# A routed-expert kernel whose residual copy of x is made from HBM to HBM, eight batches later, with SyncE's order written out

## The chip, the cores and the metric

The kernel runs on one core of a Trainium2 chip. Its time is the device time of one execution in microseconds (us). All arithmetic is in float32.

## What is computed

The input x has 32 batches of 128 tokens with 1024 channels. Two blocks follow each other, each added to its input. The first mixes the tokens of each batch with a 128x128 matrix that is looked up by the batch's condition, and sends the result through a mixture of 64 experts, 8 for each token. The second is a linear map with a low-rank adapter for each batch, followed by another linear map with a router over 8 low-rank experts.

```python
w = weights[conditions]
h = jnp.einsum('bct,bcd->bdt', x, w)
...
probs = jax.nn.softmax(h @ gate_w.T)
w, sel = jax.lax.top_k(probs, 8)
...
h = silu(einsum('ech,ehi->eci', inp, wg)) * einsum('ech,ehi->eci', inp, wu)
out = jnp.einsum('eci,eih->ech', h, wd)
y = zeros.at[tok].add(g)
...
x = x + moe(h)
x = x + L1_ffn(L1_cond(x))
```

Each expert takes at most 256 tokens. The sum x + moe(h) is what matters here: it is formed in a buffer in HBM.

## The kernel before, in words

There are three stages.

**First stage, 0 to about 283 us.** It works through the 32 batches in 8 groups of 4. For each batch `mixed` multiplies x with the looked-up matrix (two products with 512 columns, called ph), copies them to an SBUF tile h (ACT the left half, VectorE the right half), and ACT issues the write of h to the HBM buffer hbuf. For each group `scored` multiplies the turned x (xTb, loaded from a transposed copy of x) with the gate's weights (64 products, pxg), `logits` and `weights_of` choose 8 experts for each token, and `counted` ranks the tokens of each expert and writes the ranks to HBM. Between groups TensorE also works off the products of two head matrices of the last stage (`combined`, pcw): one in groups 1 to 5, two in groups 6 and 7, then nine more after the groups. During these last nine, `looked_up`, `fetched` and `found` read the ranks back (GpSimd's rkg), find the tokens of the first experts, and TensorE turns the result with a small product (prow).

The buffer ybuf is where the result x + moe(h) grows. It first gets x: `carried(b)` (L373) writes the tile of x of batch b, which is in SBUF for `mixed`, to ybuf. ACT issues this, one batch after the batch's product. Rows past the last token of hbuf, ybuf and ranks get pads: zeros and a constant, written by ACT after group 0.

The tiles: x has 6 buffers, so `loaded_batch(b + 6)` (L330) uses the buffer of batch b. xTb has 4 buffers, one group: `scored(g)` (L342) issues the loads of group g + 1. h has 3.

**Second stage, to about 2146 us.** For each of the 64 experts the kernel loads wg, wu and wd (1.5 MB each), gathers the tokens' rows of hbuf, forms the expert with a scheme of seven products in place of eight (t and s are sums of blocks of weights and tokens), and adds the weighted outputs to the rows of ybuf by an indirect DMA that accumulates.

**Third stage.** The rest of the head products (pcw with WB_b), sums of the combined map BM on VectorE, and then 16 pairs of batches: ybuf is read back (xq), turned (X), multiplied, and the output is written.

**What sets the order.** The program is written with a tile framework. A scheduler orders the instructions of an engine by its own estimate of when they are ready, except those that went through `kept` (L196): these stay in the order of the program. The class `InOrder` (L200) wraps an engine so that all of its instructions are kept. Before, VectorE, TensorE, ACT and GpSimd have such a wrapper (`dve`, `pe`, `act`, `pool`, L208), and SyncE has none: its DMA issues are placed by the scheduler. Instructions that wait hold up everything behind them on their engine. The DMAs that SyncE and ACT issue use eight completion semaphores in turn, so a DMA is issued only when the one that used the semaphore before it has landed.

Of the kernel before, what the change touches and what calls it, by code (L numbers as in the profile page):

```python
# [17 lines left out]
P = 128  # L18
NB = 32
# [32 lines left out]
def kernel(  # L52
# [22 lines left out]
    nc = tc.nc  # L75
# [8 lines left out]
    ybuf = dram.tile([NT + P, H], F32, name="ybuf")  # L84
# [90 lines left out]
    def head_block(n):  # L175
        lo, hi = BLOCKS[n]
        hw = wts.tile([P, HC * BW], F32, name=f"hw_{n}", tag="wg")
        hw = hw[:, 0 : HC * (hi - lo)].rearrange("p (j o) -> p j o", j=HC)
        nc.sync.dma_start(hw, head_w[:, lo:hi].rearrange("(j p) o -> p j o", p=P))
        return hw  # L180

    def left_block(u, k, tag):
        wb = wts.tile([P, 3, HC, P], F32, name=f"WB_{u}_{k}", tag=tag)
        nc.sync.dma_start(wb, WB[:, 3 * k : 3 * k + 3, :, :])
        return [wb[:, d, :, :] for d in range(3)]

    def multiplied(n, d, hw, left, pool, tag, pe):
# [17 lines left out]
            op = getattr(self.engine, name)  # L205
            return lambda *args, **kw: kept(op(*args, **kw))  # L206

    dve, pe, act, pool = (InOrder(e) for e in (nc.vector, nc.tensor, nc.scalar, nc.gpsimd))  # L208

# [21 lines left out]
    def fetched(some, count):  # L233
        if some["rk"] is None:
            some["rk"] = fs.tile(
                [P, some["n"] * NJ, 2, P], F32, name=f"rkg_{some['u']}", tag="rkg", bufs=2
            )
        for s in range(some["got"], some["got"] + count):
            kept(
                nc.gpsimd.indirect_dma_start(  # L240
                    out=some["rk"][:, s, :, :].rearrange("p i t -> p (i t)"),
                    out_offset=None,
                    in_=ranks.rearrange("e b i t -> (e b) (i t)"),
                    in_offset=bass.IndirectOffsetOnAxis(
                        ap=some["row"][:, s // NJ, s % NJ : s % NJ + 1], axis=0
                    ),
                )
            )
        some["got"] += count
# [67 lines left out]
    with (  # L317
# [6 lines left out]
        xs, xTs, ws = {}, {}, {}  # L324

        def loaded_turned(b):
            xTs[b] = a6.tile([P, HC, P], F32, name=f"xTb_{b}", tag="xTb", bufs=4)
            nc.sync.dma_start(xTs[b].rearrange("p j c -> p (j c)"), x_t[b])

        def loaded_batch(b):  # L330
            ws[b] = a6.tile([P, P], F32, name=f"w_{b}", tag="w_b")
            pool.indirect_dma_start(
                out=ws[b],
                out_offset=None,
                in_=cond_w,
                in_offset=bass.IndirectOffsetOnAxis(ap=cond_rows[:, b : b + 1], axis=0),
            )
            xs[b] = a6.tile([P, H], F32, name=f"x_{b}", tag="x_t")
            nc.sync.dma_start(xs[b], x[b])


        def scored(g):  # L342
            pxg = pa_sm.tile([P, GB, E], F32, name=f"pxg_{g}", tag="sm")
            for t in range(GB):
                xT_b = xTs.pop(g * GB + t)
                for j in range(HC):
                    pe.matmul(
                        pxg[:, t, :],
                        xT_b[:, j, :],
                        gw_sb[:, j, :],  # L350
                        start=(j == 0),
                        stop=(j == HC - 1),
                    )
            xg = a2.tile([P, GB, E], F32, name=f"xg_{g}", tag="xg")
            dve.tensor_copy(xg, pxg)
            for b in range((g + 1) * GB, min((g + 2) * GB, NB)):
                loaded_turned(b)
            return xg

        def mixed(b):  # L360
            rows = slice(b * P, (b + 1) * P)
            h_sb = a2.tile([P, H], F32, name=f"h_{b}", tag="h_sb", bufs=3)
            for n in range(2):
                cols = slice(n * 512, (n + 1) * 512)
                ph = pa_big.tile([P, 512], F32, name=f"ph_{b}_{n}", tag="big")
                pe.matmul(ph, ws[b], xs[b][:, cols], start=True, stop=True)
                if n == 0:
                    act.copy(h_sb[:, cols], ph)
                else:
                    dve.tensor_copy(h_sb[:, cols], ph)  # L370
            act.dma_start(hbuf[rows, :], h_sb)

        def carried(b):  # L373
            act.dma_start(ybuf[b * P : (b + 1) * P, :], xs.pop(b))

        def logits(g, xg):
            plog = pa_sm.tile([P, GB, E], F32, name=f"plog_{g}", tag="sm")
            for t in range(GB):  # L380
                pe.matmul(plog[:, t, :], ws[g * GB + t], xg[:, t, :], start=True, stop=True)
            top = a2.tile([P, GB, K], F32, name=f"top_{g}", tag="top")
            left = a2.tile([P, GB, E], F32, name=f"left_{g}", tag="left")
            for t in range(GB):
                dve.max(top[:, t, :], plog[:, t, :])
                dve.match_replace(left[:, t, :], top[:, t, :], plog[:, t, :], LOW)
            nmax = a2.tile([P, GB], F32, name=f"nmax_{g}", tag="nmax")
            dve.tensor_scalar(nmax, top[:, :, 0], -1.0, None, ALU.mult)
            ex = a2.tile([P, GB, E], F32, name=f"ex_{g}", tag="ex")
            for t in range(GB):  # L390
                act.activation(ex[:, t, :], plog[:, t, :], AF.Exp, bias=nmax[:, t : t + 1])
            mask = a2.tile([P, GB, E], F32, name=f"mask_{g}", tag="mask")
            dve.tensor_scalar(mask, left, LOW, None, ALU.is_equal)
            return ex, mask

        def weights_of(g, ex, mask):
            wt = a2.tile([P, GB, E], F32, name=f"wt_{g}", tag="wt")
            dve.tensor_tensor(wt, ex, mask, ALU.mult)
            wsum = a2.tile([P, GB], F32, name=f"wsum_{g}", tag="wsum")
            dve.tensor_reduce(wsum, wt, AX.X, ALU.add)  # L400
            rsum = a2.tile([P, GB], F32, name=f"rsum_{g}", tag="rsum")
            dve.reciprocal(rsum, wsum)
            dve.tensor_tensor(wt, wt, rsum.unsqueeze(2).to_broadcast([P, GB, E]), ALU.mult)
            return wt
# [22 lines left out]
        def combined(n, d):  # L427
            lo, hi = BLOCKS[n]
            halves = multiplied(n, d, hws[n], lefts, pa_big, "big", pe)
            next(halves)  # L430
            yield
            pcw = next(halves)
            if d < HC:
                cw = fs.tile([P, BW], F32, name=f"cw_{n}_{d}", tag="cw", bufs=3)[:, 0 : hi - lo]
                act.copy(cw, pcw)
                act.dma_start(cwbuf[:, d, lo:hi], cw)
            else:
                act.copy(G_sb[:, lo:hi], pcw)
            yield

        gw_sb = a1.tile([P, HC, E], F32, name="gw_sb")
        loaded_turned(0)
        nc.sync.dma_start(gw_sb.rearrange("p j e -> p (j e)"), gate_w)
        for b in range(1, GB):
            loaded_turned(b)
        for b in range(6):
# [8 lines left out]
        NG = NB // GB  # L455
# [4 lines left out]
        for g in range(NG):  # L460
            ex, mask = logits(g, xg)
            for t in range(GB):
                b = g * GB + t
                mixed(b)
                if b:
                    carried(b - 1)
                if t == 1:
                    wt = weights_of(g, ex, mask)
                if b + 6 < NB:
                    loaded_batch(b + 6)  # L470
            if g == 0:
                for buf in (hbuf, ybuf):
                    act.dma_start(
                        buf[NT : NT + P, :].rearrange("p (n c) -> p n c", c=256),
                        zeros.unsqueeze(1).to_broadcast([P, H // 256, 256]),
                    )
                act.dma_start(ranks[:, NB, :, :], pad)
            for _ in range((0, 1, 1, 1, 1, 1, 2, 2)[g]):
                for _ in combined(*rest.pop(0)):
                    pass  # L480
            if g + 1 < NG:
                xg = scored(g + 1)
                if g == 0:
                    lefts += left_block("a", 1, "wd")
                    lefts += left_block("a", 2, "wu")
                if g == 4:
                    hws[1] = head_block(1)
            counted(g, mask, wt)
        part = {0: looked_up([0, 1, 2, 3])}
        fetched(part[0], 4 * NJ)  # L490
        carried(NB - 1)
        gathers = {}
        for d in range(HC + 1):
            step = combined(1, d)
# [419 lines left out]
    hw = head_block(2)  # L914
# [54 lines left out]
    for q in range(NQP):  # L969
# [18 lines left out]
        o = [c3.tile([P, H], F32, name=f"out{t}_{u}", tag=f"out{t}", bufs=2) for t in range(2)]  # L988
# [105 lines left out]
```

## Time and profile before

| what | value |
|---|---|
| median of 3 runs | 2776.29 us (2773.67 to 2780.71) |
| profiled execution: time, span | 2778.05 us, 2776.3 us |
| TensorE busy | 2733.0 us, 98% |
| VectorE, ACT, GpSimd busy | 57%, 15%, 40% |
| bytes moved | 585.10 MB, mean 211 GB/s |
| load of x: issues, size, time to landing | 32, 512 KB, 7.1 us |
| write of x to ybuf | 32, 512 KB, 7.8 us |
| pads of hbuf and ybuf, time to landing | 17.4 and 19.5 us |

A profile shows one execution. The span is the time between its first and last record; the execution's own time is 1.75 us longer. Busy times of an engine are shares of this span, but matmuls are pipelined and the end of one is modelled, so a busy TensorE can be one that runs at a lower clock. "PEclk" is the clock granted to TensorE, in tenths. "DMA" is the mean busy share of the 16 DMA engines. PE is TensorE's matmul, PEld its weight load, DVE VectorE, POOL GpSimd, SP SyncE; SPq and ACTq are issues of DMAs on these engines' queues. A bracket at the end of a line gives the idle time before the instruction and what ended it.

### The profile page before, as it was taken

The numbers are of one execution on the slowest core, as the hardware profiler recorded it, in microseconds if no ns is written. First come the engines' busy times: TensorE is split into PE (matmuls) and PEld (weight loads), VectorE is DVE, ScalarE is ACT, GpSimd is POOL, SyncE is SP. The second block draws the span as 40 slices with busy tenths as digits, with TensorE's granted clock in tenths as the row PEclk, the third lists the DMA queues.
The fourth block names the chain that finished last, engine by engine and source line by source line (L and its number), as shares of the span: only waits on it lengthen the run. The fifth ranks groups of instructions, "written<-read, shape, count | busy, mean of one in ns | idle before, by whom it ended". The sixth has DMA issues, their size and how long they took to land.

```text
span 2776.3 us, 23659 instructions
## 1 busy us (share of the span) xinstructions
PE 2733.0 (98%) x8580; PEld 1515.0 (55%) x8580; DVE 1580.4 (57%) x2521; ACT 408.1 (15%) x792; POOL 1110.6 (40%) x846
## 2 busy tenths in 40 slices
PE   8899999999999999999999999999999899999999
PEld 5666555555555555555555555555555555555554
DVE  2225667666676665766757667576563444444443
ACT  1111111111111111111111111112111000000000
POOL 2114465564655646556465565555451100000000
PEclk9899999999999999999999999999999999999999
DMA  9996687777887778777777787777775522222210
GB/s 348 379 388 231 227 253 253 237 249 229 252 258 229 249 236 249 253 229 247 248 244 248 233 248 254 238 244 238 236 251 154 132 67 62 65 63 60 63 46 38
DMA packets 134724, 585.10 MB, mean 211 GB/s; under 512 B 23312, under 2 KB 50000, under 8 KB 109264
## 3 DMA queue, kind: packets, MB, share of 16 engines
q1 hardware_dynamic: 70112, 388.40, 37.9%
q0 software_dynamic: 51200, 155.24, 24.1%
q10 hardware_dynamic: 13296, 39.95, 3.7%
q8 instruction: 68, 1.11, 0.2%
q14 instruction: 48, 0.39, 0.0%
HBM read 459.68 MB, written 123.83 MB: 210 GB/s over the span
## 4 chain that ended last, share of the span: by engine, by line
PE 94%; DMA 3%; DVE 1%; issue 1%; ACT 0%; ACTq 0%; SPq 0%; POOL 0%; DVEq 0%; POOLq 0%
PE pp L591 41%; PE po L690 23%; PE pr_c L206 17%; PE pcw L206 4%; PE px L206 2%; PE pxg L206 2%; PE pth L641 2%; PE ph L206 1%; DMA xTb<-in_x_t 1%; DMA ybuf<-zeros 1%; PE prk L206 1%; DMA ybuf<-x 1%; DMA wu<-in_wu 0%; PE pg L206 0%; PE pt L206 0%
## 5 line engine op out<-in xcount | busy, mean ns | idle before, releaser
L304 POOL DMA_INDIRECT xin<-hbuf,slot_row x512 | 711.8, 1390 | 156.0 <-issue 152.7
L690 PE MATMUL po<-wd,hTb 128*128 128x512 f32 x1536 | 680.3, 592 | 0.6 <-ACT hTb L643 0.6
L701 POOL DMA_INDIRECT ybuf<-o,slot_tok x128 | 205.2, 1603 | 674.4 <-ACT o L699 472.3
L690 PEld LDWEIGHTS po<-wd,hTb 128*128 128x128 f32 x1536 | 286.8, 190 | 323.6 <-issue 306.1
L591 PE MATMUL pp<-wg,xT 128*128 128x384 f32 x1024 | 351.5, 486 | 0.0
L591 PE MATMUL pp<-t,s 128*128 128x384 f32 x1024 | 342.0, 487 | 0.0
L591 PEld LDWEIGHTS pp<-t,s 128*128 128x128 f32 x1024 | 193.5, 190 | 141.9 <-issue 23.0
L206 DVE TENSOR_TENSOR u<-p,pp 128x384 f32<-128x384 f32 x64 | 35.4, 553 | 392.0 <-PE pp L591 381.8
L591 PEld LDWEIGHTS pp<-wg,xT 128*128 128x128 f32 x1024 | 189.7, 190 | 118.9
L699 ACT ACTIVATE o<-po,slot_w 128x512 f32<-128x512 f32 x256 | 175.9, 687 | 494.2 <-PE po L690 492.1
L206 POOL DMA_INDIRECT ab<-in_AT,adapter_rows x32 | 36.5, 1142 | 447.3 <-ACT pxw L206 441.9
L206 PE MATMUL pr_c<-BM,X 128*128 128x512 f32 x480 | 213.7, 592 | 0.0
L206 DVE STREAM_TRANSPOSE xT<-xin 128x1024 f32<-128x1024 f32 x128 | 155.5, 1232 | 62.1 <-DMA xin<-hbuf,slot_row 53.5
L591 PE MATMUL pp<-wu,xT 128*128 128x384 f32 x512 | 175.6, 486 | 0.0
L591 PE MATMUL pp<-t,xT 128*128 128x384 f32 x512 | 175.6, 486 | 0.0
L591 PE MATMUL pp<-wu,s 128*128 128x384 f32 x512 | 175.6, 486 | 0.0
L608 ACT ACTIVATE h<-gate 128x384 f32<-128x384 f32 x128 | 67.0, 524 | 700.5 <-DVE gate L206 700.4
L240 POOL DMA_INDIRECT rkg<-ranks,row x128 | 123.3, 964 | 88.0 <-DMA ranks<-rk 49.3
L206 PE MATMUL pr_c<-ts,ss 128*128 128x512 f32 x320 | 142.5, 592 | 1.3 <-DVE ss L206 1.3
L206 PEld LDWEIGHTS pr_c<-BM,X 128*128 128x128 f32 x480 | 88.9, 190 | 100.2 <-issue 99.9
L206 DVE TENSOR_TENSOR u<-u,pp 128x384 f32<-128x384 f32 x128 | 70.5, 551 | 125.0 <-PE pp L591 124.9
L591 PEld LDWEIGHTS pp<-wu,xT 128*128 128x128 f32 x512 | 97.3, 190 | 67.8
(158 smaller groups left out, 2924.7 us busy)
## 6 DMA issues: line engine op xcount, KB each, us to landing
wu<-in_wu SPq DMA_DIRECT2D x64, 1536.0 KB, 9.6
wg<-in_wg SPq DMA_DIRECT2D x64, 1536.0 KB, 6.9
wd<-in_wd SPq DMA_DIRECT2D x64, 1536.0 KB, 6.9
xTb<-in_x_t SPq DMA_DIRECT2D x32, 512.0 KB, 7.6
x<-in_x SPq DMA_DIRECT2D x32, 512.0 KB, 7.1
hbuf<-h ACTq DMA_DIRECT2D x32, 512.0 KB, 8.2
ybuf<-x ACTq DMA_DIRECT2D x32, 512.0 KB, 7.8
xq<-ybuf SPq DMA_DIRECT2D x64, 256.0 KB, 5.1
```

Source lines behind the costliest of these rows:

```text
L206: return lambda *args, **kw: kept(op(*args, **kw))
L240: nc.gpsimd.indirect_dma_start(out=some["rk"][:, s, :, :].rearrange("p i t -> p (i t)"), out_offset=None, in_=ranks.rearrange("e b i t -> ...
L304: nc.gpsimd.indirect_dma_start(out=xin[:, q, :], out_offset=None, in_=quarters, in_offset=bass.IndirectOffsetOnAxis(ap=slot_row[:, s : s + ...
L591: nc.tensor.matmul(bank, left[k][:, j, :], right[k][:, j, :], start=(j == 0), stop=(j == HH - 1))
L608: nc.scalar.activation(h, gate, AF.Sigmoid)
L641: nc.tensor.transpose(pt[:, i, :], h[:, i * P : (i + 1) * P], ident)
L690: nc.tensor.matmul(po, hT[j][:, i, :], wd_sb[:, i, cols], start=(i == 0), stop=(i == IC - 1),)
L699: nc.scalar.mul(o_sb[:, cols], po, slot_w[:, s : s + 1])
L701: nc.gpsimd.indirect_dma_start(out=ybuf, out_offset=bass.IndirectOffsetOnAxis(ap=slot_tok[:, s : s + 1], axis=0), in_=o_sb, in_offset=None ...
```

## The change

`carried(b)` no longer writes the SBUF tile: SyncE issues a DMA that copies x[b] in HBM to the rows of ybuf in HBM. The compiled form of one copy is 16 rows of 32 KB each. The tile of x in SBUF then has only the two products as readers. The call moves from one batch after the product to eight batches after, behind the load of batch b + 6; the last eight follow after the groups. The pads are written after group 6 (NG - 2) instead of group 0. SyncE gets an `InOrder` wrapper, and the loads of the turned x, of x, of the gate's weights, of the head blocks and of the WB blocks go through it. The loads of wg, wu and wd, of the small constants, of pxw, BM, xq and the output writes stay outside it.

```diff
-        nc.sync.dma_start(hw, head_w[:, lo:hi].rearrange("(j p) o -> p j o", p=P))
+        sync.dma_start(hw, head_w[:, lo:hi].rearrange("(j p) o -> p j o", p=P))
...
-        nc.sync.dma_start(wb, WB[:, 3 * k : 3 * k + 3, :, :])
+        sync.dma_start(wb, WB[:, 3 * k : 3 * k + 3, :, :])
...
-    dve, pe, act, pool = (InOrder(e) for e in (nc.vector, nc.tensor, nc.scalar, nc.gpsimd))
+    dve, pe, act, pool, sync = (
+        InOrder(e) for e in (nc.vector, nc.tensor, nc.scalar, nc.gpsimd, nc.sync)
+    )
...
-            nc.sync.dma_start(xTs[b].rearrange("p j c -> p (j c)"), x_t[b])
+            sync.dma_start(xTs[b].rearrange("p j c -> p (j c)"), x_t[b])
...
-            nc.sync.dma_start(xs[b], x[b])
+            sync.dma_start(xs[b], x[b])
...
         def carried(b):
-            act.dma_start(ybuf[b * P : (b + 1) * P, :], xs.pop(b))
+            sync.dma_start(ybuf[b * P : (b + 1) * P, :], x[b])
...
-        nc.sync.dma_start(gw_sb.rearrange("p j e -> p (j e)"), gate_w)
+        sync.dma_start(gw_sb.rearrange("p j e -> p (j e)"), gate_w)
...
                 mixed(b)
-                if b:
-                    carried(b - 1)
                 if t == 1:
                     wt = weights_of(g, ex, mask)
                 if b + 6 < NB:
                     loaded_batch(b + 6)
-            if g == 0:
+                if b >= 8:
+                    carried(b - 8)
+            if g == NG - 2:
                 for buf in (hbuf, ybuf):
                     act.dma_start(
                         buf[NT : NT + P, :].rearrange("p (n c) -> p n c", c=256),
...
         fetched(part[0], 4 * NJ)
-        carried(NB - 1)
+        for b in range(NB - 8, NB):
+            carried(b)
         gathers = {}
```

The instruction lists of the two kernels agree on TensorE, VectorE and GpSimd. ACT loses the 32 writes of x, SyncE gains 32 copies. On SyncE's queue four loads of x now stand ahead of four loads of turned x in every group; 15 copies stand one after the other behind the last load of x; the second head block moves behind the turned x of group 6, expert 0's wu behind its wg and the copies; and in the third stage the third WB_b block moves from ahead of the pxw and BM loads to behind them.

## The prediction

> **What bounds the kernel now.** I read the slices of the page first, then busy times cut at the group boundaries of the first stage, then the waits of SyncE's queue, then the order of time at the two places where another engine holds TensorE.
>
> ```profile
> PE   8899999999999999999999999999999899999999
> ...
> PEclk9899999999999999999999999999999999999999
> DMA  9996687777887778777777787777775522222210
> GB/s 348 379 388 231 227 253 253 237 249 229 252 258 229 249 236 249 253 229 247 248 244 248 233 248 254 238 244 238 236 251 154 132 67 62 65 63 60 63 46 38
> ```
>
> One slice is 69.4 us. In the first three the DMA engines are full and TensorE is not; later TensorE is full and the DMAs have room. Only the first 240 us and one dip (slice 32, near 2180 us) can give anything back.
>
> Cut where each group's logits begin (columns: stretch, length, then busy us and instructions of PE, PEld, DVE, ACT, POOL; TensorE's clock, DMA share, GB/s):
>
> ```profile
> 21.00:42.80 21.80, 20.57 (x106) 14.76 (x106) 7.67 (x27) 3.16 (x8) 3.84 (x4) 1.00 0.79 286
> 42.80:78.50 35.70, 30.14 (x124) 20.80 (x125) 6.70 (x23) 5.85 (x13) 3.77 (x4) 0.81 1.03 417
> 78.50:113.30 34.80, 27.84 (x126) 21.06 (x124) 7.50 (x28) 4.80 (x11) 3.89 (x4) 0.80 1.00 392
> 113.30:136.20 22.90, 22.90 (x128) 16.52 (x126) 7.77 (x29) 4.79 (x11) 3.89 (x4) 1.00 0.92 334
> 136.20:163.80 27.60, 26.00 (x122) 18.73 (x121) 7.20 (x26) 4.80 (x11) 3.90 (x4) 0.88 1.00 386
> 163.80:186.30 22.50, 22.50 (x122) 15.81 (x120) 7.50 (x27) 4.27 (x11) 3.89 (x4) 1.00 1.02 390
> 186.30:214.40 28.10, 28.10 (x142) 19.63 (x141) 7.50 (x27) 5.71 (x13) 1.88 (x2) 1.00 0.89 346
> ```
>
> These are groups 0 to 6. Group 5, with one head product and no stall, takes 22.5 us: that is TensorE's own price of a group. Group 1 takes 13.2 us more, group 2 12.3, group 4 5.1: 30.6 us lost, with the DMA share at 1.0. Group 6 has two head products (5.2 us more) and loses nothing.
>
> The waits of SyncE's queue from 20 to 160 us (total, times, longest), and TensorE's place of waiting in group 2:
>
> ```profile
> SPq L339 <- DMA ybuf<-x: 57.2, 10, 10.8
> ...
> 102.08 7.09 PE L206 MATMUL pxg<-gw_sb,xTb 128*128 128x64 f32 x32 [6.96 <-DMA xTb<-in_x_t]
> ```
>
> SyncE stands still for 57 us because the next load of x (L339) may not overwrite a tile of x until that tile has been written to ybuf. Behind it in the same queue stand the turned tiles xTb, which TensorE then lacks.
>
> Two places where order decides, the end of the first stage and the seam before the last:
>
> ```profile
> 235.09 0.46 ACTq L206 DMA_DIRECT2D ranks<-rk  x1
> ...
> 248.60 0.39 PE L206 MATMUL prow<-byq,spread 128*128 128x8 f32 x2 [0.49 <-DVE byq L206]
> ```
> ```profile
> 2146.66 0.33 SPq L184 DMA_DIRECT2D WB_b<-in_WB  x1
> ...
> 2157.84 4.09 SPq L921 DMA_DIRECT2D BM<-cwbuf  x4
> ...
> 2169.55 6.46 DVE L206 SCALAR_TENSOR_TENSOR BM<-chan,own,BM 128x640 f32<-128x640 f32 x8 [6.79 <-DMA BM<-cwbuf]
> ...
> 2184.93 7.38 PE L206 MATMUL px<-pxw,X 128*128 128x152 f32 x32 [12.49 <-issue]
> ```
>
> From the last ranks write to the prow product nothing is spare (0.49 us already lost). At the seam TensorE idles 12.49 us behind VectorE, which waited 6.79 us for BM.
>
> **What the Trainium skill says.** "DMA: Bandwidth & Descriptors", section "Issuing engines are not separate DMA queues": transfers started by SP, ACT and POOL run on the same 16 engines and interleave; the trace agrees (417 GB/s with three queues active, no more). So moving the copy from ACT to SP frees no bandwidth by itself. Same page, "Queues, rings and completion order": an engine alternates between queues packet by packet; no run here shows it. Same page, "Latency and other measured facts", row on HBM row pitch: copies between HBM tensors at full rate are given as 214 GB/s per direction. The trace of before has no copy from HBM to HBM; I use this as the dear bound.
>
> **The change part by part.**
>
> *Price of one copy.* 512 KB is 524,288 B. At the 400 GB/s of the full stretches (mean of 417, 392, 386, 390 is 396) it takes 1.31 us of all 16 engines, whether SBUF or HBM is read. Dear bound: 524,288 B / 214 GB/s = 2.45 us. Cheap bound: the new copy is laid out as 16 rows of 32 KB instead of 128 of 4 KB; the fullest stretch moved 417 GB/s, which would be 1.26 us. I take 1.31: reading x from HBM is what its load does and writing ybuf is what the old copy did, and both ran at full rate.
>
> *Tile of x free sooner.* The 57.2 us of SyncE's wait vanish: a tile of x is free when its two products are done. Next are TensorE's products themselves and the eight completion slots that SP and ACT share; both come sooner than a write that took 7.8 us to land.
>
> *Bytes put off.* When logits of group 3 began (113.3 us), 41.7 MB had moved (the first stretch 331 x 21.0, then 286 x 21.8, 417 x 35.7, 392 x 34.8). In it were 11 copies (5.8 MB) and the zero pads (1.05 MB). In the new order only 4 copies stand there: 9 us less at 400 GB/s, to which the order adds: xTb of the next group no longer stands behind loads of x that wait for a write. Bytes that scored of group 3 needs in the new order: x 0 to 13 (7.3), xTb 0 to 15 (8.4), head and WB_a (6.3), h 0 to 11 (6.3), the rest 1.7: 30 MB. 12.3 MB are in by 40 us as before; 17.7 MB / 400 GB/s = 44 us, so 84 us, and TensorE's own pace gives 42.8 + 22.5 + 22.5 = 88. TensorE sets it: 113.3 becomes 88 to 95.
>
> *Groups 3 to 6.* A group then moves x, xTb, h and copies at 2.1 MB each plus 0.7: 9.1 MB, 22.8 us at 400 GB/s against TensorE's 22.5: balanced. By the scored of group 7: 68 MB, 40 + 55.7/0.39 = 183 us, against TensorE's 88 + 22.5 x 3 + 28.1 = 184. So logits of group 7 could begin at 184 instead of 214.4. Two limits this close never both hold, and the shared slots tie loads to landings of h: I take a third of the 30.6 us as not recovered. Gain 20 us.
>
> *The end of the stage.* After the last load of x (its tile is free in group 6) SyncE issues 15 copies without a wait on an engine: 7.9 MB, 20 us, into DMA time that was 11 to 28% free, with h 26 to 31 and the pads (4 MB, 10 us): from about 180 to 212 us. The last ranks write would come near 215; it finds a short tail of them. Its 5.5 us landing may become 8, and each us there stalls prow: 0 to 5, taken 3 us lost. The pads, now after group 6 on ACT's queue, took 17.4 and 19.5 us to land; a head-product write behind them shares a slot with one, and ACT's copies of rk stand behind that. TensorE has scored and counted (9.6 us) and the second head product before it needs those: some 20 us of cover, so 0, up to 5 if the cover is short.
>
> *Loads moved back.* The second head block (SP at 109.6 us) goes behind xTb of group 6, expert 0's wu (at 126.5) behind the copies, after wg. Their readers are the second head's first product (TensorE, 234.9 us) and VectorE (263.5 us), some 20 us earlier in the new run. Both loads still have 25 us or more: 0. ACT loses 32 issues; it was busy 15%: 0.
>
> *The seam.* The written order puts the third WB_b after BM: pxw no longer waits for the wd buffer until 2146.66, and BM finds a ring without 1.5 MB and pxw ahead of it. BM lands 2 to 4 us sooner, VectorE and TensorE follow: gain 3 us (0 to 4). WB_b then lands near 2173; its reader comes after 2197.
>
> *Sum.* -20 + 3 - 3 = -20 us on the profiled execution: 2776.3 span (2778.05 with what lies around it) to 2756 (2758). The median shown is 2776.29, 1.8 below the profiled time; the same step gives 2756.
>
> **Rivals.**
> 1. *Balanced, little regained* (about 2772). The stage is limited by DMA bytes nearly everywhere, the total of 85 MB is unchanged, and copies at 1.8 us cost 17 x 0.5 = 8 us more before group 7, the pads' stall comes back in group 6 with 5, the ranks tail costs 3: -20 + 16 = -4. For it: shares of 1.0. Against: groups 5 and 6 held TensorE's pace at 390 and 346 GB/s.
> 2. *Copies from HBM to HBM run at half rate* (about 2788, slower). At 2.45 us the 17 copies before group 7 cost 19 us more, so logits there gain some 6 us only. The 15 last copies take 37 us instead of 20 and still run when ranks is written; ranks and the gathers from it alternate with 32 KB pieces, and prow has no cover: 18 us late. -6 + 18 = +12. It decides once a copy takes over 1.75 us: 15 x 1.75 = 26 us is what fits between the last load of x and the last ranks write beside 10 us of other traffic.
> 3. *Full recovery* (about 2744): all 30.6 us and the seam, no tail.
>
> That the copy or the order isn't what is said can be left out: the instruction lists show 32 copies on SP, none on ACT, TensorE, VectorE and POOL unchanged.
>
> **How the numbers follow.** Forecast 2756: 0.50. Full recovery: 0.12. Balanced: 0.24. Half rate: 0.14. The low end is 2743, full recovery; the high end 2779 takes in the balanced case with both tail costs and leaves out most of the half rate. A measurement here tells about 0.3% (8 us) from no change. Faster 0.62, within 0.24, slower 0.14.
>
> **What would show it.** SyncE's wait at the load of x on a write of ybuf gone; groups 1 and 2 at 23 to 27 us and the clock there near 1.00; logits of group 7 near 190 to 195; a copy landing in under 10 us with the DMA at 390 GB/s or more; prow waiting under 4 us; the px wait at the seam near 9.5 us. The forecast is wrong if copies hold the rate near 214 GB/s, if h waits for its writes behind 32 KB pieces, or if a group's loads stay tied to landings through the slots.

## The result, and the profile after

The changed kernel takes 2768.91 us (median of 11 runs, 2765.91 to 2772.56), the kernel before in the same comparison 2776.91 us: ratio 0.9974, 95% interval 0.9964 to 0.9983, 8 us faster. The forecast was 20 us faster, 2756 us, in a range of 2743 to 2779. The profiled execution took 2768.09 us, its span is 2766.4 us; all differences below are between it and the one of before (2776.3).

The slices of the page, for the kernel after (69.2 us each). TensorE's dip has moved from the second slice to the fourth, 207 to 277 us, which is the end of the first stage; DMA moves more there (263 GB/s, before 231), and less in the third:

```profile
PE   8998999999999999999999999999999899999999
...
DMA  9997777777878878777787777777775522222210
GB/s 349 381 376 263 238 255 227 248 262 225 251 241 243 255 225 252 256 234 248 235 249 254 229 247 253 241 244 238 237 248 153 137 74 62 62 61 65 60 43 38
```

The first stage cut where each group's logits begin, groups 0 to 6 (same columns as before: stretch, length, PE, PEld, DVE, ACT, POOL, clock, DMA share, GB/s):

```profile
20.90:40.90 20.00, 19.96 (x106) 14.79 (x107) 6.60 (x23) 4.12 (x10) 3.85 (x4) 1.00 0.77 273
40.90:71.30 30.40, 28.02 (x124) 21.09 (x123) 7.59 (x27) 4.79 (x12) 3.78 (x4) 0.83 1.02 416
71.30:93.90 22.60, 22.60 (x124) 16.22 (x123) 7.49 (x27) 4.82 (x12) 3.91 (x4) 1.00 1.00 393
93.90:116.50 22.60, 22.60 (x124) 16.22 (x123) 7.49 (x27) 4.82 (x12) 3.91 (x4) 1.00 0.96 360
116.50:140.40 23.90, 23.25 (x123) 16.44 (x123) 7.50 (x27) 4.83 (x12) 3.90 (x4) 1.00 1.01 391
140.40:163.20 22.80, 22.80 (x123) 16.28 (x122) 7.49 (x27) 4.83 (x12) 3.91 (x4) 1.00 1.01 387
163.20:198.00 34.80, 32.73 (x140) 23.76 (x139) 7.51 (x27) 5.30 (x13) 1.89 (x2) 0.85 0.97 379
```

Groups 2 and 4, which had lost 12.3 and 5.1 us, run within 1.4 us of TensorE's own pace (22.5), group 1 keeps 7.9 of its 13.2. Logits of group 6 begin at 163.2 instead of 186.3: 23 us gained. Then group 6 takes 34.8 us instead of 27.9, so that 16.2 are left at the logits of group 7 (198.0 against 214.2). That last step belongs to this execution more than to the change: of six other kernels below whose queues on SyncE and ACT agree with this one up to these logits, five took 27.8 to 28.3 us in group 6 and one 34.6, and group 7 began at 188.1 to 207.1.

The waits of SyncE's queue from 20 to 160 us no longer hold an entry at the load of x for a write of the old copy. What stands in its place are shared completion semaphores ("slots" below), whose last user is a write of h or of ranks:

```profile
SPq L206 <- DMA hbuf<-h: 55.5, 18, 9.6
SPq L206 <- DMA ranks<-rk: 19.3, 4, 7.0
```

Later, from 160 to 290 us, one such slot is that of the late pad of ybuf:

```profile
SPq L206 <- DMA ybuf<-zeros: 5.8, 1, 5.8
```

The last load of x waits for it until 191.01, and the row of 15 copies stands behind that load.

The end of the stage, in order of time over all engines (rkg is GpSimd's read of the ranks, hit VectorE's first use of it). First the kernel before:

```profile
241.45 0.94 POOL L240 DMA_INDIRECT rkg<-ranks,row  x1 [49.33 <-DMA ranks<-rk]
...
245.54 0.43 DVE L206 TENSOR_TENSOR hit<-rkg,rank 128x256 f32<-128x256 f32 x1 [6.19 <-DMA rkg<-ranks,row]
...
248.84 5.46 PE L206 MATMUL pcw<-hw,WB_a 128*128 128x388 f32 x16
```

The kernel after:

```profile
191.39 24.72 SPq L206 DMA_DIRECT2D ybuf<-in_x  x15
...
207.88 0.33 ACTq L206 DMA_DIRECT2D hbuf<-h  x1
...
218.27 0.58 ACT L206 COPY rk<-prk 64x512 f32<-64x512 f32 x1 [0.29 <-PE prk L206]
...
222.92 0.45 ACTq L206 DMA_DIRECT2D ranks<-rk  x1
...
226.50 0.38 SPq L557 DMA_DIRECT2D wg<-in_wg  x1
226.91 0.95 POOL L242 DMA_INDIRECT rkg<-ranks,row  x1 [58.00 <-DMA cwbuf<-cw]
226.92 0.43 SPq L560 DMA_DIRECT2D wu<-in_wu  x1
...
235.90 0.42 DVE L206 TENSOR_TENSOR hit<-rkg,rank 128x256 f32<-128x256 f32 x1 [12.78 <-DMA rkg<-ranks,row]
...
238.94 0.59 PE L206 MATMUL prow<-byq,spread 128*128 128x8 f32 x2 [7.04 <-DVE byq L206]
...
239.38 8.05 PE L206 MATMUL pcw<-hw,WB_a 128*128 128x388 f32 x16
```

The ranks are ready at 218.85 (218.27 + 0.58) and are written at 222.92 only. The slot that they got was that of the last write of h: issued at 207.88, among the copies, it landed after 15.0 us, at 222.85; the eight writes of h in the kernel before from 186 to 230 us took 2.6 to 8.3. The last copy, issued at 215.63, landed at 225.2. The reader starts 4.0 us after the write of ranks (before: 6.4), and its first result is used 9.0 us after that (before: 4.1), beside the 3 MB of wg and wu. TensorE idles 7.04 us (before: 0.49), and the 16 products after that take 8.05 us, at a granted clock of 0.67, where the kernel before needs 5.46. Stage 2 begins at 277.13 instead of 283.26: of the 16.2 us only 6.1 are left.

The seam before the third stage:

```profile
2148.11 4.71 SPq L924 DMA_DIRECT2D BM<-cwbuf  x4
...
2152.93 1.77 SPq L206 DMA_DIRECT2D WB_b<-in_WB  x1
...
2159.95 6.45 DVE L206 SCALAR_TENSOR_TENSOR BM<-chan,own,BM 128x640 f32<-128x640 f32 x8 [4.22 <-DMA BM<-cwbuf]
...
2175.32 6.65 PE L206 MATMUL px<-pxw,X 128*128 128x152 f32 x32 [9.92 <-issue]
```

BM is now asked for at 2148.11, before the third WB_b, and VectorE waits 4.22 us for it instead of 6.79. TensorE idles 9.92 us instead of 12.49. With 1.2 us in stages 2 and 3 that makes 9.9 us in the span.

### The profile page after: what moved, and what is told of

It is laid out like the page before. It is cut to its first block, busy times and chain, and to the rows that moved or that the text cites. A ratio compares the mean times of both kernels' runs of the same rounds, so it can differ in the third digit from the quotient of the medians.

```text
span 2766.4 us, 23669 instructions
## 1 busy us (share of the span) xinstructions
PE 2729.5 (99%) x8580; PEld 1513.0 (55%) x8580; DVE 1581.5 (57%) x2521; ACT 408.6 (15%) x792; POOL 1123.1 (41%) x846
## 4 chain that ended last, share of the span: by engine, by line
PE 96%; DMA 2%; DVE 1%; issue 0%; ACT 0%; SPq 0%; POOL 0%; ACTq 0%; DVEq 0%
PE pp L594 42%; PE po L693 23%; PE pr_c L206 17%; PE pcw L206 4%; PE px L206 2%; PE pxg L206 2%; PE ph L206 2%; PE pth L644 2%; DMA xTb<-in_x_t 1%; DMA hbuf<-h 1%; PE prk L206 1%; PE plog L206 0%; DMA rkg<-ranks,row 0%; PE pg L206 0%; PE pt L206 0%
## 5 line engine op out<-in xcount | busy, mean ns | idle before, releaser
L306 POOL DMA_INDIRECT xin<-hbuf,slot_row x512 | 722.6, 1411 | 159.2 <-issue 151.8
```

The source lines that it names most:

```text
L306: nc.gpsimd.indirect_dma_start(out=xin[:, q, :], out_offset=None, in_=quarters, in_offset=bass.IndirectOffsetOnAxis(ap=slot_row[:, s : s + ...
```

## The experiments

All were timed beside the kernel before; ratios are to it. "Logits", "prow" and "stage 2" are start times in the one profiled execution of a kernel; before they are 214.2 (group 7), 248.6 and 283.3, after 198.0, 238.9 and 277.1. Since group 7 began anywhere from 188.1 to 207.1 us in seven kernels whose queues agree up to it, a few us at these logits say nothing of an edit.

### One part of the change at a time

**The source alone.** The kernel before, ACT issuing at the old place, but from HBM:

```diff
-            act.dma_start(ybuf[b * P : (b + 1) * P, :], xs.pop(b))
+            act.dma_start(ybuf[b * P : (b + 1) * P, :], x[b])
```

> The kernel before with one edit: the copy reads x in HBM instead of the SBUF tile; ACT issues it at the old place, pads early, no wrapper. Theory (the tile of x that is free sooner is half of what the first groups gained, the bytes put off are the other half): groups 1 and 2 recover 10 of 25 us, but with the bytes unchanged the groups after them stay limited by DMA; nothing is piled up at the end, so prow waits under 2 us. 2768 to 2772 us. Rival (only the bytes put off count): within 3 us of 2776.9.

Measured: 2778.32 us, ratio 1.0003 (0.9995 to 1.0011). Logits 215.8, prow 249.6. A tile of x that is free sooner is worth nothing as long as the same bytes go out at the same place and hold the same slots; this run doesn't tell the two apart. With the copies read from HBM, groups 1 and 2 moved 406 and 414 GB/s, so the new source is as fast as the old one.

**The order alone.** The kernel before with the `InOrder` wrapper on SyncE, copies from SBUF by ACT:

```diff
-            nc.sync.dma_start(xs[b], x[b])
+            sync.dma_start(xs[b], x[b])
```
(and the same at the other four loads of the change)

> The kernel before with SyncE's order written out and nothing else: ACT still writes the tile of x to ybuf, pads after group 0. In the first stage SyncE's list is then the same as before; what moves is the third WB_b block, behind pxw and BM at the seam. Theory (the written order acts at the seam alone): px waits 9 to 10 us instead of 12.5, 2772 to 2774, the first stage unchanged (logits of group 7 at 212 to 216). Rival (the order also acts in the first stage): logits of group 7 move by over 5 us and the time leaves 2770 to 2776.

Measured: 2824.68 us, ratio 1.0175 (1.0162 to 1.0188): 49 us slower. The rival had said that the order acts in the first stage too, but nobody had a loss of this size. SyncE's queue in this kernel:

```profile
104.27 28.75 SPq L206 DMA_DIRECT2D x<-in_x  x4
133.11 4.93 SPq L206 DMA_DIRECT2D xTb<-in_x_t  x4
138.15 31.70 SPq L206 DMA_DIRECT2D x<-in_x  x4
```

Four loads of x stand ahead of four turned tiles. Each waits for a write of its tile to ybuf (130.9 us in 16 waits up to 290 us), so the four take some 30 us to issue and the turned tiles come late in every group: group 1 takes 43.3 us, groups 2 to 5 take 36 to 37, and the clock falls to 0.72 to 0.75 there. The expectation took SyncE's first-stage list to be that of before; in fact the scheduler had put loads of x between the turned tiles, and the written order undid that. So this order is good only with a copy that doesn't hold the tile. The seam did as the theory said (px waits 9.82 us).

**The copy and the pads without the written order.** The changed kernel with `sync = nc.sync`:

> SyncE's wrapper is taken away; its instruction list then differs from the changed kernel's only in the third WB_b block, which goes back ahead of pxw and BM. Theory (the seam gained 3.3 us by it, and nothing else comes from the written order): 2772 us, the px wait at the seam back at 12 to 12.5 us, first stage unchanged. Rival (the seam's gain is from something else): 2769 us and a wait near 10 us.

Measured: 2773.29 us, ratio 0.9985 (0.9979 to 0.9992). With copies from HBM the scheduler makes the first stage's list of the changed kernel by itself; only the third WB_b goes back ahead of pxw and BM. px waits 12.60 us again. The written order is worth 4 us by the medians, 3 by the ratios; 2.7 of them are seen at the seam, the rest is not located.

**All but the late pads.**

```diff
-            if g == NG - 2:
+            if g == 0:
```

> Only the pads go back behind group 0; all else is as in the changed kernel (2768.9 us). Theory (bytes at the end of the stage: group 6 lost 6.6 us because the DMA engines were full, and the pads are 1.05 MB of it; the ranks' way lost 9.5 us to wg, wu and the last copies): group 6 shortens by some 3 us, group 0 or 1 grows by 2 to 5 where the DMA engines are as full, so 2768 to 2772 us in all, and the wait of prow stays near 7 us. Rival (the pads are what the end of the stage paid for): group 6 falls to 28 us and the whole to about 2762 us.

Measured: 2777.54 us, ratio 0.9999 (0.9992 to 1.0005): the whole gain is gone. Neither side had this. (The profiled execution, 2773.18 us, is one of the fast ones and shows half of the loss: stage 2 at 281.2.) SyncE's queue, this kernel first, the changed kernel second:

```profile
32.79 19.13 SPq L206 DMA_DIRECT2D x<-in_x  x4
52.02 3.08 SPq L206 DMA_DIRECT2D xTb<-in_x_t  x4
...
82.33 12.44 SPq L206 DMA_DIRECT2D xTb<-in_x_t  x4
```
```profile
33.97 7.68 SPq L206 DMA_DIRECT2D x<-in_x  x4
45.05 11.68 SPq L206 DMA_DIRECT2D xTb<-in_x_t  x4
...
70.05 4.18 SPq L206 DMA_DIRECT2D xTb<-in_x_t  x4
```

The pads take 15.4 and 16.9 us to land and hold slots for so long; one load of x stands 8.3 us for such a slot (waits of SyncE's queue, 20 to 110 us):

```profile
SPq L206 <- DMA ybuf<-zeros: 8.3, 1, 8.3
```

Four loads of x take 19 us to issue instead of 8, the next turned tiles start 12 us late, the DMA share falls to 0.85 to 0.89 from 60 to 120 us (351, 300 and 333 GB/s), and that hole isn't made up.

**The same pads, as early, from GpSimd.** Is it the slots, or the small pieces (1 KB) on the DMA engines?

```diff
-            if g == NG - 2:
+            if g == 0:
...
-                    act.dma_start(
+                    pool.dma_start(
```
(the pad of ranks likewise)

> The changed kernel with the pads after group 0 again, issued by GpSimd instead of ACT, so that the same bytes in the same 1 KB pieces move at the same place, but no completion slot of ACT and SyncE stands behind them. Theory (it is the slots and the waiting on them): groups 1 and 2 as in the changed kernel (30.4 and 22.6 us), 2768 to 2772. Rival (it is the slow small pieces on the DMA engines): group 1 near 37 us and 2775 to 2779, as with the pads on ACT.

Measured: 2765.66 us, ratio 0.9963 (0.9950 to 0.9976), as good as the changed kernel. From 60 to 120 us DMA moves 416, 388 and 393 GB/s; group 2 takes 22.6 us (group 1 30.9). SyncE's 8.3 us at a pad's slot are gone. Same bytes, same pieces, same place: what the copies need is that no slot shared by ACT and SyncE stands behind the pads. The pads also landed sooner from GpSimd (8.7 and 13.0 us); no run takes this apart from the slots. The Trainium skill ("DMA: Bandwidth & Descriptors", "Issuing engines are not separate DMA queues") says that issuing from several engines saves only the time on the sequencer. Here the choice of engine is worth the difference of the two ratios, 0.36% or 10 us, because a slow DMA from ACT keeps a slot that SyncE's loads need; the bandwidth itself is no more, as the page says (416 GB/s in group 1 of the changed kernel too).

**The late pads alone**, in the kernel before:

> The kernel before with the pads after group 6 and nothing else. With the changed copy, taking the pads back cost the whole gain (9 us). Theory (the pads cost a hole in the DMA early on, because ACT and SyncE stand behind their landing; in the kernel before, the load of x waits for the write of ybuf there anyway, so the hole is hidden): 2773 to 2777, logits of group 2 no more than 4 us sooner (74 to 78). Rival (the pads cost 9 us wherever the rest stands): 2767 to 2769, logits of group 2 near 70.

Measured: 2783.10 us, ratio 1.0027 (1.0016 to 1.0038), 7 us slower; logits of group 2 at 79.6, of group 7 at 217.8. The theory had 2773 to 2777 and logits of group 2 at 74 to 78, so it missed the number; what it said of the cause holds as far as it goes: nothing is gained where loads of x wait for writes of ybuf anyway (99.6 us of such waits up to 290 us, 91.5 before); the DMA was full in group 1 with the pads (417 GB/s) and without (419). Why it is slower is not settled: SyncE's list comes out a little different from the scheduler, and groups 1 and 4 take 1.2 and 3.7 us more.

### Where the rest of the forecast went

**Expert 0's wg and wu later**, away from the read of the ranks. ACT issues them behind the second head's third product:

```diff
             if d == 2:
+                gate0 = loaded_gate(0, act)
                 found(part[0], 0, 1)
```
(`loaded_gate` issues the two loads; `loaded(0)` takes over what it returns.)

> Only expert 0's wg and wu move: ACT issues them behind the second head's third product, after the ranks were read, instead of SyncE just ahead of the read. Theory (wg and wu, 3 MB, collide with the read of the ranks): rkg lands in 3 to 4 us again, prow waits 2 to 3 us instead of 7, the clock dip there goes, and the time falls by 5 to 7 us to about 2763 us. Rival (the delay is the shared completion slots and the copies' backlog): prow waits 6 to 7 us as before and the time stays within 2 us of 2768.9.

Measured: 2768.53 us, ratio 0.9969 (0.9957 to 0.9981), no change. Logits of group 7 came at 191.5, but the ranks, ready at 213.24, stood until 224.19 for the slot of the last write of h, and prow came at 241.6 after 16.23 us idle. ACT issued wg at 226.49 all the same, beside the read. The kernel without the written order shows the same: logits 190.7, prow 237.9 after 13.24 us idle. Whenever group 7 starts, prow comes near 238 to 242. From this came a new theory: the last ranks write goes out only when the copies queued ahead of it are through.

**Eight copies more** (batches 0 to 7 again, behind the last eight; work that is not needed):

> Batches 0 to 7 are copied a second time behind the last copies (the same data once more): 8 copies and 4.2 MB more ahead of the ranks, TensorE's work unchanged. New theory (bytes): each copy costs 4.2 MB / 8 / 0.4 = 1.31 us, the ranks go 8 to 10.5 us later, prow waits 15 to 17 us instead of 7, and the time is 2777 to 2780 us. Rival (the end is hidden or set by something else): under 2772 us.

Measured: 2771.33 us, ratio 0.9989 (0.9980 to 0.9997): 2.4 us over the changed kernel by the medians, 4 by the ratios, not 10. SyncE issues 23 copies in one row from 187.9 to 228.1; ACT's ranks write takes its slot at 220.51 among them, 10.6 us after the ranks were ready, and the copies behind it slow only the read (12.3 us to its first use, wg and wu issued only for its last 3). Prow did wait 17.77 us, as the theory had it, but group 7 had begun at 188.1, so that prow came at 239.8, no later than after the change. What costs is what stands ahead of the ranks, or beside the read, not the total.

**The last eight as one DMA**, 64 rows of 64 KB. Is it the number of slots, or the bytes?

```diff
-        for b in range(NB - 8, NB):
-            carried(b)
+        sync.dma_start(ybuf[(NB - 8) * P : NB * P, :].rearrange("(k r) h -> k (r h)", k=128), x[NB - 8 : NB].rearrange("b (k r) h -> (b k) (r h)", k=16))
```

> The last 8 copies are issued as one DMA of 4 MB (64 rows of 64 KB): the same bytes, 7 completion slots fewer. New theory (bytes): within 3 us of 2768.9, prow near 238. Rival (slots: what delays the ranks is that their DMA waits for the slot of a copy): the ranks are issued when rk is copied, at 218 us, prow waits under 4 us, and the time falls by 4 to 6 us.

Measured: 2769.78 us, ratio 0.9973 (0.9963 to 0.9984), no change. The ranks were issued at 220.78, the moment they were copied (220.75), as the rival had it; but the write then took 11.0 us to land, and prow came at 244.6 after 13.26 us idle. So seven slots fewer buy nothing: without the wait for a slot, the write itself is slow behind the same bytes. (Their pieces are larger here; no run takes that apart.)

**The last eight behind expert 0's wd**:

```diff
-        for b in range(NB - 8, NB):
-            carried(b)
...
         mine = loaded(0)
+        for b in range(NB - 8, NB):
+            sync.dma_start(ybuf[b * P : (b + 1) * P, :], x[b])
```
(expert 0's three loads go through `sync` to keep this order)

> The last 8 of the 15 copies that SyncE issues in one row move behind expert 0's wd, which waits for TensorE until about 244 us, so they run after the ranks were read. New theory (the ranks of the last group are written only when the bytes ahead of them are through, some 82 MB, at 222 to 224 us, however early logits of group 7 begin): 8 x 1.31 = 10 us fewer bytes stand ahead, the ranks are written near 214 to 218 us, prow follows near 230, and the time falls by 7 to 9 us to about 2760 us. Rival (shared completion slots or wg and wu in the way): prow stays near 238 and the time within 2 us of 2768.9.

Measured: 2761.77 us, ratio 0.9949 (0.9935 to 0.9963). The interval lies just below that of the changed kernel (0.9964 to 0.9983): this beats both. Its end of the stage:

```profile
213.92 0.33 SPq L206 DMA_DIRECT2D wg<-in_wg  x1
...
216.42 0.45 ACTq L206 DMA_DIRECT2D ranks<-rk  x1
225.77 0.94 POOL L242 DMA_INDIRECT rkg<-ranks,row  x1 [52.65 <-DMA cwbuf<-cw]
...
233.30 0.59 PE L206 MATMUL prow<-byq,spread 128*128 128x8 f32 x2 [3.86 <-DVE byq L206]
...
239.43 17.11 SPq L206 DMA_DIRECT2D ybuf<-in_x  x8
```

The ranks go out as soon as they are copied (215.81 + 0.58), and stage 2 starts at 271.3, 5.8 us sooner than after. What is left: the write now stands beside wg and wu, and 9.35 us pass until its reader starts (4.0 after).

**All of the last 16 behind wd**:

> All 16 copies of the second half of x move behind expert 0's wd; no copy is issued from the last load of x until then. New theory (bytes): nothing is piled up ahead of the ranks, TensorE's own pace from logits of group 7 (191 us) to prow (34.4 us later) is what is left, prow near 226 to 230 with a wait under 3 us, and the time at 2756 to 2759 us; the 21 us of copies then lie beside the first gathers with the DMA engines at 0.6 and cost under 2 us. Rival (slots, or wg and wu): within 2 us of the run with 8 moved.

Measured: 2772.93 us, ratio 0.9989 (0.9981 to 0.9998). Stage 2 starts at 262.8, 14.4 us sooner than after, and by the last head products the gain is down to 0.9 us (2138.51 against 2139.44). SyncE issues 16 copies from 230.9 to 260.2, and expert 1's loads come after them: its wd goes out at 261.24, its wu at 268.5, to land 17.1 us later. VectorE waits 14.34 us for that wu, and TensorE idles 10.08 us before 288.60. The bytes are only moved on, into a place that needs its own.

**The last eight behind wd, and wg and wu late**:

> The last 8 copies behind expert 0's wd, as in the run at 2761.8, and expert 0's wg and wu issued by ACT behind the second head's third product, so that neither copies nor these 3 MB stand beside the last write of ranks and the reads of it. Theory (what is left of prow's wait, 3.9 us, is the time that the ranks spend beside wg and wu): from the ranks' issue to the read's start 4 to 5 us instead of 9.4, prow waits under 1 us, start of stage 2 sooner by about 4 us, 2757 to 2761, if wg and wu still land before VectorE's sums need them. Rival (the ranks take as long whatever runs beside them): prow waits 3 to 5 us, 2761 to 2764.

Measured: 2764.62 us (2753.63 to 2774.09), ratio 0.9949 (0.9935 to 0.9962); the runs of this kernel lie far apart, and the profiled one (span 2772.4) is the slowest, with logits of group 7 at 207.1. For the way of the ranks alone it can be read:

```profile
228.00 0.45 ACTq L214 DMA_DIRECT2D ranks<-rk  x1
232.52 0.94 POOL L250 DMA_INDIRECT rkg<-ranks,row  x1 [54.14 <-DVE row L214]
...
236.76 0.42 DVE L214 TENSOR_TENSOR hit<-rkg,rank 128x256 f32<-128x256 f32 x1 [4.51 <-DMA rkg<-ranks,row]
...
240.86 0.28 PE L214 MATMUL prow<-byq,spread 128*128 128x8 f32 x2
```

From the ranks write to prow 12.9 us, against 16.9 with wg and wu beside it, 16.0 after and 13.5 before; prow waits for nothing. So in these two executions the 3 MB cost the ranks 4 us. The theory's gain in time (2757 to 2761) was not seen: the third prow waits 2.59 us instead, with wg and wu now beside the reads that follow, and the spread of the runs covers the rest.

## Why the prediction was wrong

Point by point, by its steps, with the working not told again:

- *Price of a copy*, 1.31 us: right. With copies in the mix the full groups (2, 4 and 5) moved 387 to 393 GB/s, and a copy took 8.3 us to land. (An estimate: at half rate, 2.1 of a group's 9.1 MB would have cost double, 9.1 / 11.2 of 390, or 317 GB/s.) The row of 214 GB/s in the Trainium skill ("DMA: Bandwidth & Descriptors", "Latency and other measured facts") was measured on tiles of 128 rows of 16 KiB; as a bound for these copies of 16 rows of 32 KB it doesn't hold, and the rival built on it is refuted.
- *Tile of x free sooner, and bytes put off*: the mechanism is right; the source alone gave nothing, and the later place alone was not run. Logits of group 3 came at 94.0, inside "88 to 95". (The "9 us less" there counts the seven copies only; the pads, 1.05 MB, would add 2.6. As TensorE set the time, nothing hung on it.) 23 us were gained by the logits of group 6, three quarters of the 30.6; the 7.5 missing are nearly all group 1's. At the logits of group 7 the profiled execution has 16.2 us, not 20, and 198 instead of "190 to 195"; the seven kernels with the same queues up to there have 7 to 26 us, 18.7 in the middle one. So the 20 us were about right.
- *The end of the stage*, "from about 180 to 212 us ... it finds a short tail of them ... taken 3 us lost": this step failed. The copies took 34 us, close to the 32 reckoned, but from 191.4 to 225.2: they start behind the last load of x, and that stood for the slot of a pad until 191.0. (The two times of the step don't belong together: copies from 180 fit a group 7 at 184, with nothing lost, and ranks at 215 one at 194, with a third lost.) So the ranks, ready at 218.9, found not a short tail but a slot held 4.1 us by a write of h that took 15.0 us among the copies (the last write of h took 4.8 us with eight of them behind wd and 2.6 with 16). The loss measured 10.1 us (16.2 at the logits of group 7, 6.1 at the start of stage 2): 6.55 more idle at prow, 2.6 in the slow products behind it, 0.9 elsewhere. The 6.55 are 4.0 more until the write of ranks is issued and 4.9 more at the read, less 2.4 that the read followed the write sooner. Undoing it (last eight behind wd) gives back 7 us of the median.
- *Loads moved back*, "both loads still have 25 us or more: 0": failed too. Their readers had time; but the loads were given a new place beside the ranks read, which has none: its first result took 9.0 us instead of 4.1. The pair of runs with and without the two beside it shows 4 us.
- *Pads*: at their new place they landed in 10.8 and 14.3 us and cost TensorE nothing that shows, as priced. But they held SyncE 5.8 us ahead of the copies, which the step had not looked at; what that is worth was not measured. What was not seen either is their worth at the old place: 7 us by the ratios and 9 by the medians with the new copy, none with the old. They were reckoned as bytes; it is what stands behind them.
- *The seam*: right; 3 forecast, 2.6 measured at px, 3 to 4 in the time of the run without the order.

The rival "balanced, little regained" (2772) came nearest in the number, but not for its reason: copies didn't cost 1.8 us each, and the groups did regain their time.

So 8 instead of 20: most of the stalls went, as said, and then the bytes that were put off (the 85 MB of the stage are the same) came due ahead of the one write that everything waits for. The profiled executions show it side by side (us):

| kernel | logits of group 7 | prow | stage 2 | logits to stage 2 |
|---|---|---|---|---|
| before | 214.2 | 248.6 | 283.3 | 69.1 |
| changed | 198.0 | 238.9 | 277.1 | 79.1 |
| changed, no written order | 190.7 | 237.9 | 275.3 | 84.6 |
| wg and wu late | 191.5 | 241.6 | 278.9 | 87.4 |
| eight copies more | 188.1 | 239.8 | 277.9 | 89.7 |
| last eight as one | 197.2 | 244.6 | 281.6 | 84.4 |
| last eight behind wd | 195.5 | 233.3 | 271.3 | 75.8 |
| last 16 behind wd | 190.3 | 227.4 | 262.8 | 72.5 |
| last eight behind wd, wg and wu late | 207.1 | 240.9 | 280.7 | 73.6 |

With all copies ahead of the ranks, prow comes at 238 to 245 whenever group 7 begins, so what group 6 won or lost was spent there anyway. With eight or 16 of them behind, the stretch from the logits to stage 2 shortens towards that of the kernel before. That the step at the end is to blame is shown by these runs. Why group 6 lost 6.9 us in two of the seven executions is only read from the trace (full DMA, loads of the turned x behind landings of h); no run took it apart.

## What to carry to other kernels

Putting bytes off moves a bottleneck; it doesn't shrink it. Ask what stands behind them in the queue where they land, above all short writes and reads that the next stage hangs on, and put the deferred bytes behind those, in portions that the next stage can carry (8 copies gained 7 us, 16 gave it back). The parts of such a change are not a sum: source alone 0, order alone 49 us slower, late pads alone 7 us slower, all together 8 us faster, and all but the late pads nothing; so test the parts against the whole, not against the kernel before alone.

## What was not expected of the hardware

- A DMA of 512 KB in pieces of 1 KB (512 of them) took 15.4 and 16.9 us to land when ACT issued it and 8.7 and 13.0 us when GpSimd did, both at 33 us into the changed kernel with the DMA share at 1.03. Issued by ACT at 208 us into the kernel before, with the share at 0.90, it took 7.3 and 7.9. A copy of the same size from HBM to HBM, in 32 KB rows, took 8.3 in the median.
- A small read by indirect DMA (the ranks) took 4.1 to 4.2 us from its start to its first use without those loads, 9.0 us beside the 3 MB of wg and wu, and 12.3 with eight more copies beside it.
- A write of 512 KB (h) from ACT took 15.0 us to land among the copies that SyncE had queued, and 2.6 to 8.3 in the kernel before at the same place.
- After 7 us of idling TensorE's 16 products took 8.05 us instead of 5.46, at a granted clock of 0.67; after 3.9 us (last eight behind wd) 7.89. A wait can cost more than its length.
